# Two-layer image kernel on one core: the norm of image 1 over two rows, its mask additions over three, the last sums of image 0 ahead of the exponentials, and the residual load in the row before

## Chip, core and metric

One NeuronCore of one Trainium2 chip runs the whole batch. The metric is the device time of one launch in microseconds (us). Three runs of the kernel before give 3633.53, 3634.03 and 3636.36 us; the median is 3634.03. The profile comes from one more execution, 3639.9 us from first to last instruction (its own time is 3641.7 us).

## What is computed

The input is 32 images of 56 x 56 positions and 128 channels, float32. Two layers follow each other, each added to its own input:

```python
x = x + window_attention(group_norm(x))
x = x + fourier_ff(group_norm(x))
```

`group_norm` takes mean and variance of groups of 4 channels over a whole image. The attention cuts the image, rolled by 3 in both directions, into 8 x 8 windows of 7 x 7 positions, with 4 heads of 32; to the scores it adds a bias by relative position and a mask (-100 between regions) that differs only in the last window row and the last window column. `fourier_ff` takes a cosine transform along each axis, keeps 32 modes, mixes channels mode by mode, transforms back, adds both axes, and applies a feed-forward net of 128 -> 512 -> 128 with relu.

## The kernel before

**Work units.** An image has 8 rows of windows. The kernel's clock is the "cycle": cycle r handles window row r of the stream of 32 x 8 rows. In one cycle the attention stages of several rows stand side by side: queries and keys of row r (`attn_qk`), scores and maximum of row r, exponential and division, transposes of an earlier row, values of row r-3, projection of row r-3 (`attn_project`, which also adds the input and sends the row to a scratch tensor in DRAM), and sums of a row for the second norm (`attn_sums`). Three cycles behind the end of an image its second layer starts: statistics (`fourier_stats`), transforms, mixing, back transforms, and the feed-forward net in 7 groups of tokens at cycles 8, 9, 10, 12, 13, 14, 15 of that image (`FF_AT`), so that it runs beside the attention of the next image. The first 11 cycles (`CONV_BEGIN`) have attention only; they run through `first_rows` (L956). All later ones run through `halves_first`, `eighths`, `quarters`, `full`, `halves_last`.

**Order.** PE, ACT, DVE and POOL execute in the order in which the code is written (`tc.manual_schedule`, L999), except the setup ahead of it. SP, which issues nearly all DMAs, is ordered by a scheduler, not by the text. Buffers come from rotating pools: the attention has 4 PSUM banks (`pa`), handed out in turn, so that a matmul group waits for whoever empties the bank used four groups earlier.

**The places that the change touches.**

- `bias_and_mask(r)` (L187 to L198): 16 DVE additions of 49 x 98 that build `bm`, the table of bias plus mask. r = 0 is built at setup, r = 1 (only used by the last window row, cycle 7) in cycle 1 (L984), after the maximum of that cycle.
- `image_norm` (L315 to L368) is a generator: each `next` runs it to the next `yield`. Its pieces are: statistics on DVE and the power -0.5 on POOL (L333 to L356); the small product `nb` on DVE and the scaled weights `wn` on ACT (L358 to L362); two PE matmuls of one column that wait for `nb`, and the DVE copy of their result into `bqkv` (L364 to L367). For image 0 all of it runs ahead of cycle 0 (L1003). For image 1 all of it runs in cycle 6 (three calls in `first_rows`); for every later image in cycle 7 of the image before.
- `attn_sums` (L557): a DVE sum over `xl`, an ACT square, a DVE sum over the squares. In cycle 10 the sums of row 7 of image 0 come after `attn_exp` and `attn_divide` (L990 to L993). `fourier_stats` (L579) begins cycle 11: a DVE sum `tot` over all rows' sums, then PE matmuls with `gmean`, then a short DVE chain, then a POOL power `rstd` (L616), which ACT needs to evict the transforms (L653).
- `ff_in` (L738): allocates `res` (two buffers), issues its load from the scratch tensor (L744, L748), adds the bias `b2sb` to it on POOL (L751), then runs the first half of the feed-forward net. `ff_out` (L766) adds its result to `res` on DVE and issues the output.
- `image_bias` (L301) adds `bproj` to the image on POOL, two instructions in each of cycles 0 to 3.

Of the kernel before, what the change touches and what calls it, by code (L numbers as in the profile page):

```python
# [10 lines left out]
F32 = mybir.dt.float32  # L11
# [37 lines left out]
def swin_fourier_kernel(  # L49
# [36 lines left out]
    def conv_bank():  # L86
        return bank("pc", 4)
# [96 lines left out]
    nc.gpsimd.memset(bm, 0.0)  # L184
    rpb_f = rpb.rearrange("p (t u) y x -> p t u (y x)", u=2)

    def bias_and_mask(r):  # L187
        for t in range(2):
            for half in range(2):
                rows = slice(half * JP, half * JP + WT)  # L190
                for k, p0, p1 in ((0, 0, NP - half), (1, NP - half, NP)):
                    for p in range(p0, p1):
                        nc.vector.tensor_tensor(
                            bm[rows, r, t, p],
                            rpb_f[rows, t],
                            mask_sb[rows, r, k].unsqueeze(1).to_broadcast([WT, 2, WT]),
                            ALU.add,
                        )  # L198

    bias_and_mask(0)  # L200
    dct_w = const_load([TC, 2 * NM], dct, "dct_w")
    dct_h = const.tile([TC, 2 * NM], F32, tag="dct_h", name="dct_h")
    for r in range(0, TC, S):
# [111 lines left out]
    def image_norm(im):  # L315

        GR = C // 16

        def average(out, src):
            sums = small.tile([P, GR], F32, tag="gsums", name="gsums", bufs=2)  # L320
            nc.vector.tensor_reduce(
                sums, src.rearrange("p (g c) -> p g c", c=4), axis=AX.X, op=ALU.add
            )
            nc.vector.tensor_scalar(
                out.rearrange("p (g c) -> p g c", c=4),
                sums.unsqueeze(2).to_broadcast([P, GR, 4]),
                0.25,
                None,
                ALU.mult,
            )  # L330

        yield
        nc.vector.bn_aggr(stat[:, 0:2], im.st)  # L333

        turned = small.tile([P, 32], F32, tag="turned", name="turned", bufs=2)
        nc.vector.transpose(turned, stat)
        mean = small.tile([P, 2, 32], F32, tag="gmeans", name="gmeans", bufs=2)
        average(mean[:, 0], turned)
        nc.vector.tensor_tensor(turned, turned, mean[:, 0], ALU.subtract)
        nc.vector.tensor_tensor(turned, turned, turned, ALU.mult)  # L340
        average(mean[:, 1], turned)
        back = small.tile([P, 2, 32], F32, tag="back", name="back", bufs=2)
        nc.vector.transpose(
            back.rearrange("p k c -> p (k c)"), mean.rearrange("p k c -> p (k c)")
        )
        gm = back[:, 0, 0:1]

        nc.vector.tensor_scalar(im.xw[0][:, RT : RT + 1], gm, -1.0, None, ALU.mult)

        ve = small.tile([P, 1], F32, tag="ve", name="ve")  # L350
        nc.vector.scalar_tensor_tensor(
            out=ve, in0=back[:, 0, 1:2], scalar=1e-5, in1=back[:, 1, 0:1], op0=ALU.add, op1=ALU.add
        )
        rstd = small.tile([P, 1], F32, tag="rstd0", name="rstd0")
        nc.gpsimd.tensor_tensor(rstd, ve, mhalf, ALU.pow)
        im.w = work.tile([P, 3 * C], F32, tag="wn", name="wn")  # L356
        yield
        nb = small.tile([P, 1], F32, tag="nb0", name="nb0")  # L358
        nc.vector.scalar_tensor_tensor(
            out=nb, in0=gm, scalar=-1.0, in1=rstd, op0=ALU.mult, op1=ALU.mult  # L360
        )
        nc.scalar.mul(im.w, wqkv, rstd)  # L362
        yield
        pb = attn_bank()  # L364
        halved(pb[:, 0:1], wqkv[:, 2 * C :], nb)
        im.bias = small.tile([P, 5], F32, tag="bqkv", name="bqkv")
        nc.vector.tensor_copy(im.bias[:, 2:3], pb[:, 0:1])  # L367
        yield  # L368

# [365 lines left out]

    def ff_in(im, g):  # L738
        t0, n = sum(FF_GROUPS[:g]), FF_GROUPS[g]
        k, last = n // P, n % P  # L740
        xff = im.xf.rearrange("p r w -> p (r w)")
        scr_tok = im.scr.rearrange("h w c -> (h w) c")
        res = work.tile([P, 4, C], F32, tag="res", name="res")
        nc.sync.dma_start(  # L744
            res[:, :k], scr_tok[t0 : t0 + k * P].rearrange("(n p) c -> p n c", p=P)
        )
        if last:
            nc.sync.dma_start(res[:last, k], scr_tok[t0 + k * P : t0 + n])  # L748
        for c0, c1, m in ((0, k, P), (k, k + 1, last)):
            if m:  # L750
                nc.gpsimd.tensor_tensor(  # L751
                    res[:m, c0:c1],
                    res[:m, c0:c1],
                    b2sb[:m].unsqueeze(1).to_broadcast([m, c1 - c0, C]),
                    ALU.add,
                )
        im.res = res
        im.hid = []
        for f in range(NF):
            ph = conv_bank()  # L760
            halved(ph[:, :n], wff1[:, f * P : (f + 1) * P], xff[:, t0 : t0 + n])
            hf = work.tile([P, HB], F32, tag="hid", name="hid", bufs=NF)
            nc.scalar.activation(hf[:, :n], ph[:, :n], AF.Relu, bias=b1sb[:, f : f + 1])  # L763
            im.hid.append(hf)

    def ff_out(im, g):  # L766
        t0, n = sum(FF_GROUPS[:g]), FF_GROUPS[g]
# [67 lines left out]
    def load_back(cycle):  # L835
        for im, c in fourier(cycle):
            for width, g in back_groups(c):
                load_modes(im, width, g)

    def nothing():  # L840
        while True:
            yield
# [7 lines left out]
    def halves_first(cycle, norm):  # L850
        for im, c in fourier(cycle):
            if c == 0:
                im.stats = fourier_stats(im)
                im.cols = {}
                next(im.stats)
        last, j = row(cycle - 4)
        sums = attn_sums(last, j) if last and cycle > CONV_BEGIN else nothing()
        next(sums)
        im, i = row(cycle)
        if im:  # L860
            attn_qk(im, i, False)
        next(norm)
        next(sums)
        for im, c in fourier(cycle):
            if c in FF_AT:
                ff_in(im, FF_AT.index(c))
        for im, c in fourier(cycle):
            if c == 0:
                next(im.stats)

    def has_ff(cycle):
        return any(c in FF_AT for _, c in fourier(cycle))
# [54 lines left out]
    def halves_last(cycle, norm):  # L927
        im, i = row(cycle)
        if im:
            attn_v(im, i, cycle)  # L930
        if has_ff(cycle):
            half_columns(cycle)
        half_columns(cycle, True)
        load_back(cycle + 1)
        next_begin(cycle)
        load_first(cycle)
        next(norm)
        if row(cycle)[0]:
            attn_exp(cycle)
            attn_divide(cycle)  # L940
        im, j = row(cycle - 3)
        if im:
            last_out(cycle)
            attn_project(im, j)
        next(norm)

    def next_begin(cycle):
        b, i = divmod(cycle, NWR)
# [7 lines left out]
    def first_rows(cycle, norm):  # L956
        im, i = row(cycle)
        if im:
            attn_qk(im, i, True)
        if cycle:  # L960
            attn_exp(cycle - 1)
        im3, i3 = row(cycle - 3)
        if im3:
            attn_values(im3, i3, cycle - 3)
        im2, i2 = row(cycle - 2)
        if im2:
            attn_transpose(im2, i2, cycle - 2)
        if cycle:
            attn_divide(cycle - 1)
        if im:  # L970
            attn_scores(im, i, cycle)
            attn_max(cycle)
        if im3:
            attn_project(im3, i3)
        next(norm)
        last, j = row(cycle - 4)
        if last:
            for _ in attn_sums(last, j):
                pass
        if im:  # L980
            attn_v(im, i, cycle)
        if cycle < NWR // 2:
            image_bias(im, 2 * cycle)
        if cycle == 1:  # L984
            bias_and_mask(1)
        next(norm)
        next_begin(cycle)
        next_groups(cycle)
        if cycle == CONV_BEGIN - 1:
            attn_exp(cycle)  # L990
            attn_divide(cycle)
            for _ in attn_sums(im3, i3):
                pass  # L993
            last, j = row(cycle - 1)
            attn_transpose(last, j, cycle - 1)
        next(norm)

    ET = mybir.EngineType
    with tc.manual_schedule(engines={ET.PE, ET.Activation, ET.DVE, ET.Pool}):  # L999
        images[0] = image_begin(0)  # L1000
        for i in range(0, NWR, 2):
            image_groups(images[0], i)
        for _ in image_norm(images[0]):  # L1003
            pass
        norm = nothing()
        for cycle in range(NB * NWR + CONV_BEGIN + FF_AT[-1] - NWR + 1):
            if cycle < CONV_BEGIN:
                first_rows(cycle, norm)
# [16 lines left out]
                full(cycle)  # L1025
                halves_last(cycle, norm)
            b, i = divmod(cycle, NWR)
            norm = nothing()
            if i == (NWR - 2 if b else NWR - 3) and b + 1 < NB:
                norm = image_norm(images[b + 1])  # L1030
                next(norm)


# [60 lines left out]
```

## Time and profile before

| what | value |
|---|---|
| median of 3 runs | 3634.03 us (3633.53 to 3636.36) |
| profiled execution | 3639.9 us, mean granted PE clock 0.995 |
| PE busy | 3574.4 us, 98% |
| DVE / ACT / POOL busy | 2211.9 / 2148.1 / 1368.3 us (61 / 59 / 38%) |
| DMA | 390.31 MB, mean 107 GB/s |
| chain that ended last | PE 92%, DVE 4%, issue, ACT, POOL and DMA 1% each |

How to read it: the page gives totals, and then the span in 40 slices (91 us each), one digit of busy tenths for each engine, and the granted PE clock. The trace behind it can be asked for a stretch of time: the timeline lists instructions of an engine in order with the idle time ahead of each and what ended it (in brackets); the waits list who waited for whom, in total, times, longest; the table of windows gives each engine's busy time in a stretch and the granted clock. In all of them `pa L112 <- DVE nb L359` means that a PE instruction writing `pa` at line 112 waited for the DVE instruction at line 359 that wrote `nb`.

### The profile page before, as it was taken

To read this page: it belongs to the slowest core of one execution; us is meant where nothing else is said; L and a number is where in the kernel's file an instruction comes from. 1 tells how busy PE (TensorE), PEld (TensorE's weight loads), DVE (VectorE), ACT (ScalarE), POOL (GpSimd) and SP (SyncE) were. 2 spreads that over 40 slices of the span, in tenths; PEclk is the share of its full clock that TensorE was granted. 3 is DMA by queue.
4 is the path that set the end of the run, shared out by engine and by line. 5 is a ranking of instruction groups with operands and counts; after the bars stand their busy time and mean duration, and the time that the engine had idled before them with its cause. 6 is when DMAs were issued, how large, how long until landed. Compare 5 with 4: busy or idle time off the path is not lost.

```text
span 3639.9 us, 161666 instructions
## 1 busy us (share of the span) xinstructions
PE 3574.4 (98%) x72192; PEld 2832.6 (78%) x72192; DVE 2211.9 (61%) x4738; ACT 2148.1 (59%) x4044; POOL 1368.3 (38%) x1421
## 2 busy tenths in 40 slices
PE   7899999999999999999999999999999999999999
PEld 5677777778777787877777878777777777787776
DVE  7766666666666666666656656666566666565641
ACT  4555566655566555666556665556665556655553
POOL 5433333333343433333333434333333334343321
PEclk8999999999999999999999999999999999999999
DMA  4334434444434444334444344443444443444343
GB/s 114 86 102 112 113 96 111 108 110 111 112 97 112 112 109 116 94 110 107 113 108 111 94 114 109 113 114 94 111 108 111 110 111 94 114 109 109 97 115 98
DMA packets 687350, 390.31 MB, mean 107 GB/s; under 512 B 39967, under 2 KB 657600, under 8 KB 686400
## 3 DMA queue, kind: packets, MB, share of 16 engines
q1 hardware_dynamic: 686045, 379.65, 38.3%
q8 instruction: 568, 9.31, 1.1%
q14 instruction: 126, 1.03, 0.1%
q10 hardware_dynamic: 611, 0.32, 0.0%
HBM read 218.29 MB, written 161.48 MB: 104 GB/s over the span
## 4 chain that ended last, share of the span: by engine, by line
PE 92%; DVE 4%; issue 1%; ACT 1%; POOL 1%; DMA 1%; SPq 0%; POOLq 0%; DVEq 0%; ACTq 0%
PE pc L112 37%; PE pa L112 14%; PE pa L408 6%; PE pc L679 6%; PE pa L474 6%; PE pc L645 6%; PE pa L430 5%; PE pa L499 4%; PE pc L718 4%; PE pa L275 3%; DVE a L438 1%; DVE xf L729 0%; DVE oT L530 0%; POOL rstd L616 0%; ACT a L455 0%
## 5 line engine op out<-in xcount | busy, mean ns | idle before, releaser
L449 POOL TENSOR_TENSOR a<-a,mx 128x784 f32<-128x784 f32 x256 | 389.4, 1521 | 1427.3 <-DVE mx L448 1203.4
L112 PE MATMUL pc<-wff,hid 128*64 128x128 f32 x12544 | 740.3, 273 | 1.5 <-ACT hid L763 0.8
L112 PE MATMUL pc<-xf,wff 128*64 128x512 f32 (+2 forms) x3584 | 717.5, 539 | 1.1 <-DVE xf L729 1.0
L112 PEld LDWEIGHTS pc<-wff,hid 128*64 128x64 f32 x12544 | 702.6, 137 | 8.2 <-ACT hid L763 4.5
L460 DVE TENSOR_REDUCE sm<-a 128x16 f32<-128x784 f32 x256 | 248.2, 970 | 686.1 <-ACT a L455 682.8
L463 POOL TENSOR_TENSOR a<-a,rs 128x784 f32<-128x784 f32 x256 | 389.1, 1520 | 566.6 <-DVE rs L462 542.8
L763 ACT ACTIVATE hid<-pc,b1sb 128x512 f32<-128x512 f32 (+2 forms) x896 | 527.1, 632 | 76.6 <-PE pc L112 74.5
L112 PEld LDWEIGHTS pc<-xf,wff 128*64 128x64 f32 x3584 | 279.8, 137 | 368.0 <-issue 260.5
L379 ACT ACTIVATE q<-pa,bqkv 128x392 f32<-128x392 f32 x256 | 150.4, 587 | 473.1 <-PE pa L112 467.5
L112 PE MATMUL pa<-xw,wn 128*64 128x392 f32 (+1 forms) x2048 | 390.6, 497 | 3.7 <-DVE aT L484 2.7
L530 DVE TENSOR_SCALAR oT<-pa,bqkv 128x98 f32<-128x98 f32 (+2 forms) x768 | 171.0, 278 | 268.7 <-PE pa L499 268.6
L751 POOL TENSOR_TENSOR res<-res,b2sb 128x512 f32<-128x512 f32 (+2 forms) x256 | 264.2, 1037 | 113.5 <-DMA res<-scr 113.5
L408 PE MATMUL pa<-wn,xw 128*64 128x128 f32 x4096 | 283.6, 280 | 4.7 <-issue 3.5
L306 POOL TENSOR_TENSOR xl<-xl,bproj 112x512 f32<-112x512 f32 (+1 forms) x256 | 286.8, 1142 | 0.0
L499 PEld LDWEIGHTS pa<-aT,v 49*32 49x32 f32 x16384 | 172.9, 106 | 146.1 <-issue 127.0
L415 ACT COPY v<-pa 128x512 f32<-128x512 f32 x256 | 150.9, 589 | 228.3 <-PE pa L408 228.3
L438 DVE TENSOR_TENSOR a<-pa,bm 128x392 f32<-128x392 f32 x512 | 264.8, 559 | 25.8 <-PE pa L430 2.1
L455 ACT ACTIVATE a<-a 128x784 f32<-128x784 f32 x256 | 222.3, 869 | 97.2 <-POOL a L449 96.8
L482 ACT COPY aT<-pa 113x452 f32<-113x452 f32 x256 | 139.4, 544 | 210.4 <-PE pa L474 206.6
L408 PEld LDWEIGHTS pa<-wn,xw 128*64 128x64 f32 x4096 | 221.4, 137 | 38.6 <-issue 9.1
L112 PE MATMUL pa<-wproj,oT 128*64 128x128 f32 (+1 forms) x3584 | 248.0, 274 | 1.8 <-DVE oT L530 1.8
L448 DVE TENSOR_REDUCE mx<-a 128x16 f32<-128x784 f32 x256 | 246.3, 962 | 4.3
(91 smaller groups left out, 5583.8 us busy)
## 6 DMA issues: line engine op xcount, KB each, us to landing
zscr<-z SPq DMA_DIRECT2D x512, 112.0 KB
htok<-scr SPq DMA_DIRECT2D x256, 196.0 KB
zT<-zscr SPq DMA_DIRECT2D x192, 256.0 KB
res<-scr SPq DMA_DIRECT2D x160, 256.0 KB
out_dram<-res SPq DMA_DIRECT2D x160, 256.0 KB
scr<-xl SPq DMA_DIRECT2D x128, 224.0 KB
xl<-in_x_dram SPq DMA_DIRECT2D x32, 784.0 KB
xl<-in_x_dram SPq DMA_DIRECT2D x32, 672.0 KB
```

The costliest lines, as they stand in the source:

```text
L112: nc.tensor.matmul(dst[ps], lhsT=lhsT[:, ps], rhs=rhs, start=start, stop=stop)
L306: nc.gpsimd.tensor_tensor(piece, piece, bproj.unsqueeze(1).to_broadcast([TC, e - a, C]), ALU.add)
L408: nc.tensor.matmul(pv[hs, j * C : (j + 1) * C], lhsT=im.xw[i][:, w * WT : w * WT + JP], rhs=im.w[:, 2 * C : 3 * C], start=True, stop=True,)
L438: nc.vector.tensor_tensor(a[:, 2 * hp : 2 * hp + 2, :, 0:WT].rearrange("p u w j -> p w u j"), ps[hp][:, :RT].rearrange("p (w u j) -> p w u ...
L448: nc.vector.tensor_reduce(mx, a3, axis=AX.X, op=ALU.max)
L449: nc.gpsimd.tensor_tensor(a3, a3, mx.unsqueeze(2).to_broadcast([P, 2 * NWR, WT]), ALU.subtract)
L455: nc.scalar.activation(a3, a3, AF.Exp)
L460: nc.vector.tensor_reduce(sm, a3, axis=AX.X, op=ALU.add)
L463: nc.gpsimd.tensor_tensor(a3, a3, rs.unsqueeze(2).to_broadcast([P, 2 * NWR, WT]), ALU.mult)
L499: nc.tensor.matmul(po4[u][h * HD : (h + 1) * HD, 2 * f + e], lhsT=v[ks, 2 * f + e, h * HD : (h + 1) * HD], rhs=im.aT[i][f][ks, h, e * JP : ...
L751: nc.gpsimd.tensor_tensor(res[:m, c0:c1], res[:m, c0:c1], b2sb[:m].unsqueeze(1).to_broadcast([m, c1 - c0, C]), ALU.add,)
L763: nc.scalar.activation(hf[:, :n], ph[:, :n], AF.Relu, bias=b1sb[:, f : f + 1])
```

## The change

Four edits. (1) `bias_and_mask` takes a part (0 to 3, four additions each); table 1 is built by one part in cycle 1, one in cycle 2, two in cycle 3. (2) `image_norm` of image 0 is advanced three steps ahead of cycle 0, its last step (matmuls and copy) in cycle 0; of image 1, the statistics stay in cycle 6, the rest goes to cycle 7; `im.bias` is allocated earlier. (3) In cycle 10 the sums of row 7 go ahead of exponential and division. (4) `ff_in` is split: `load_residual` is called from `load_back`, which runs at the end of the cycle before; the POOL addition `ff_residual` is called at the end of `halves_first`.

```diff
-    def bias_and_mask(r):
-        for t in range(2):
-            for half in range(2):
-                rows = slice(half * JP, half * JP + WT)
...
+    def bias_and_mask(r, part):
+
+        t, half = divmod(part, 2)
+        rows = slice(half * JP, half * JP + WT)
...
-    def ff_in(im, g):
+    def load_residual(im, g):
         t0, n = sum(FF_GROUPS[:g]), FF_GROUPS[g]
         k, last = n // P, n % P
-        xff = im.xf.rearrange("p r w -> p (r w)")
         scr_tok = im.scr.rearrange("h w c -> (h w) c")
         res = work.tile([P, 4, C], F32, tag="res", name="res")
...
+        im.next_res = res
+
+    def ff_in(im, g):
...
+        im.res = im.next_res
...
+    def ff_residual(im, g):
...
@@ load_back(cycle)
                 load_modes(im, width, g)
+            if c in FF_AT:
+                load_residual(im, FF_AT.index(c))
@@ halves_first, at its end
             if c == 0:
                 next(im.stats)
+        for im, c in fourier(cycle):
+            if c in FF_AT:
+                ff_residual(im, FF_AT.index(c))
@@ first_rows
-        next(norm)
+        next(norm, None)
...
-        if cycle == 1:
-            bias_and_mask(1)
-        next(norm)
+        for part in {1: (0,), 2: (1,), 3: (2, 3)}.get(cycle, ()):
+            bias_and_mask(1, part)
+        if cycle == NWR - 1:
+            next(norm, None)
         next_begin(cycle)
         next_groups(cycle)
         if cycle == CONV_BEGIN - 1:
+            for _ in attn_sums(im3, i3):
+                pass
             attn_exp(cycle)
             attn_divide(cycle)
-            for _ in attn_sums(im3, i3):
-                pass
...
-        next(norm)
@@ main loop
-        for _ in image_norm(images[0]):
-            pass
-        norm = nothing()
+        norm = image_norm(images[0])
+        for _ in range(3):
+            next(norm)
```

More of the change, by code (lines that the diff above doesn't have):

```diff
@@ L185, in swin_fourier_kernel @@
     rpb_f = rpb.rearrange("p (t u) y x -> p t u (y x)", u=2)
-    def bias_and_mask(r):
-        for t in range(2):
-            for half in range(2):
-                rows = slice(half * JP, half * JP + WT)
[L191 to L200, printed above, removed]
+    def bias_and_mask(r, part):
+        t, half = divmod(part, 2)
+        rows = slice(half * JP, half * JP + WT)
+        for k, p0, p1 in ((0, 0, NP - half), (1, NP - half, NP)):
+            for p in range(p0, p1):
+                nc.vector.tensor_tensor(
+                    bm[rows, r, t, p],
+                    rpb_f[rows, t],
+                    mask_sb[rows, r, k].unsqueeze(1).to_broadcast([WT, 2, WT]),
+                    ALU.add,
+                )
+    for part in range(4):
+        bias_and_mask(0, part)
     dct_w = const_load([TC, 2 * NM], dct, "dct_w")
@@ L356, in image_norm @@
         im.w = work.tile([P, 3 * C], F32, tag="wn", name="wn")
+        im.bias = small.tile([P, 5], F32, tag="bqkv", name="bqkv")
         yield
@@ L365, in image_norm @@
         halved(pb[:, 0:1], wqkv[:, 2 * C :], nb)
-        im.bias = small.tile([P, 5], F32, tag="bqkv", name="bqkv")
         nc.vector.tensor_copy(im.bias[:, 2:3], pb[:, 0:1])
@@ L748, in ff_in @@
             nc.sync.dma_start(res[:last, k], scr_tok[t0 + k * P : t0 + n])
+        im.next_res = res
+    def ff_in(im, g):
+        t0, n = sum(FF_GROUPS[:g]), FF_GROUPS[g]
+        xff = im.xf.rearrange("p r w -> p (r w)")
+        im.res = im.next_res
+        im.hid = []
+        for f in range(NF):
+            ph = conv_bank()
+            halved(ph[:, :n], wff1[:, f * P : (f + 1) * P], xff[:, t0 : t0 + n])
+            hf = work.tile([P, HB], F32, tag="hid", name="hid", bufs=NF)
+            nc.scalar.activation(hf[:, :n], ph[:, :n], AF.Relu, bias=b1sb[:, f : f + 1])
+            im.hid.append(hf)
+    def ff_residual(im, g):
+        n = FF_GROUPS[g]
+        k, last = n // P, n % P
+        res = im.res
         for c0, c1, m in ((0, k, P), (k, k + 1, last)):
@@ L756, in ff_in @@
                 )
[L757 to L764, printed above, removed]
     def ff_out(im, g):
@@ L944, in halves_last @@
             attn_project(im, j)
-        next(norm)
+        next(norm, None)
     def next_begin(cycle):
@@ L974, in first_rows @@
             attn_project(im3, i3)
-        next(norm)
+        next(norm, None)
         last, j = row(cycle - 4)
@@ L983, in first_rows @@
             image_bias(im, 2 * cycle)
-        if cycle == 1:
-            bias_and_mask(1)
-        next(norm)
+        for part in {1: (0,), 2: (1,), 3: (2, 3)}.get(cycle, ()):
+            bias_and_mask(1, part)
+        if cycle == NWR - 1:
+            next(norm, None)
         next_begin(cycle)
@@ L989, in first_rows @@
         if cycle == CONV_BEGIN - 1:
+            for _ in attn_sums(im3, i3):
+                pass
             attn_exp(cycle)
             attn_divide(cycle)
-            for _ in attn_sums(im3, i3):
-                pass
             last, j = row(cycle - 1)
             attn_transpose(last, j, cycle - 1)
-        next(norm)
     ET = mybir.EngineType
@@ L1027, in swin_fourier_kernel @@
             b, i = divmod(cycle, NWR)
-            norm = nothing()
             if i == (NWR - 2 if b else NWR - 3) and b + 1 < NB:
                 norm = image_norm(images[b + 1])
-                next(norm)
+                next(norm, None)
 def _constants():
```

## The prediction

> **What bounds the kernel now.** I read three views in this order: the 40 slices, the table of windows, and PE's waits. The slices of the page show where there is anything to win:
>
> ```profile
> PE   7899999999999999999999999999999999999999
> PEclk8999999999999999999999999999999999999999
> ```
>
> Only the first two slices (182 us) have a PE that is visibly idle or below full clock. The table of windows (length, then PE busy first) puts numbers on the middle:
>
> ```profile
> 1000.00:1900.00 900.00, 894.68 (x18214) 713.40 (x18214) 555.21 (x1184) 539.07 (x1014) 343.91 (x356) 1.00 0.40 108
> 1900.00:2800.00 900.00, 896.52 (x18262) 712.71 (x18260) 557.89 (x1190) 542.94 (x1025) 343.89 (x357) 1.00 0.40 108
> ```
>
> PE is busy 99.4 to 99.6% of these at clock 1.00. So from about 204 us on PE is the bound. From 240 to 3500 us PE's waits add to 10.1 us for some 29 images. The time before 204 us holds the rest; the same waits over the whole span name the edits' places:
>
> ```profile
> PE pa L112 <- DVE nb L359: 10.3, 3, 4.7
> ...
> PE pa L112 <- DVE tot L581: 4.0, 1, 4.0
> ...
> PE pa L112 <- DVE aT L484: 2.7, 1, 2.7
> ```
>
> One long wait for each startup edit: nb (norms of images 0 and 1), tot (second norm of image 0), aT (behind the mask additions). But in this stretch DVE is nearly full too (22 to 25 us of each 30 from 30 to 120 us), so a wait of PE is worth only what DVE can follow.
>
> **What the Trainium skill says.** "SBUF — State Buffer", section "SBUF: two separate sides": a DVE instruction with two SBUF inputs and a GpSimd instruction that reads SBUF exclude each other; whoever starts first holds the shared port for its whole instruction. The mask additions (rpb and mask, both SBUF) are of this kind. The trace agrees: with POOL idle 8 took 1.48 us (24.47), 0.19 each; in cycle 1 they met POOL's L449 and L306. Chain of waits (start, length, what), then POOL's timeline:
>
> ```profile
> 33.77 3.07 DVE bm L193 x4
> 36.85 1.49 DVE bm L193 x4
> 38.36 0.77 DVE bm L193 x4
> 39.13 0.78 DVE bm L193 x4
> ```
> ```profile
> 33.92 1.57 POOL L449 TENSOR_TENSOR a<-a,mx 128x784 f32<-128x784 f32 x1 [0.38 <-DVE mx L448]
> 35.45 2.26 POOL L306 TENSOR_TENSOR xl<-xl,bproj 112x512 f32<-112x512 f32 x2
> ```
>
> The first four take 3.1 us, the last eight 0.77 per four once POOL is done at 37.7. "TensorE: Matmul & The Clock Gate", section "What's actually happening": PE falls to half clock after an idle window of about 3.4 us and is back after a busy one. Here it shows after PE's idle 4.41 us at 77.1: 77.1 to 86.9 has clock 0.53.
>
> **The change part by part.** I compared the built programs' instruction order, engine by engine.
>
> Edit 4, residual: SP has the same DMAs in the same order with the same kinds of wait before and after, because SP's order is the scheduler's, which had already put each load ahead as far as the two buffers allow (in the tail each load is issued 2.3 us after the output that frees its buffer). POOL differs only once per image: the power L616 now stands ahead of the residual addition L751 (1.28 us), which so waits for the statistics too. Waits of that power, 220 to 3500 us:
>
> ```profile
>   DVE ve L612: 54.7, 29
> ```
>
> POOL was idle for 1.9 us before each of the 29, so the addition never held it back: no gain. The addition then comes some 4 us later (428.4 for 424.74); behind it on POOL stands L449 of the next maximum, which waits another 4.4 us for DVE (at 432.80), and ff_out's DVE addition comes at 437.7. No loss. DMAs: none moves. Value 0; ends -1.2 (the only other wait of ACT's L653 for that power, 5.1 us in two, 3.9 of them in image 0) and +1.
>
> Edit 2, image 0: the two one-column matmuls leave the space before the first queries. Those start at 18.43, and wn, which they need, ends at 18.38: no gain. DVE's first mask table waits for a DMA until 24.47 anyway: 0. The two matmuls go in front of the values of cycle 0, where PE is later idle 1.05 us: 0 (ends -0.4, +0.7).
>
> Edit 1, mask additions. Cycle 1 keeps 4 instead of 16: DVE goes on at 36.84 instead of 39.95, -3.1. DVE's timeline from there, before:
>
> ```profile
> 42.86 0.97 DVE L448 TENSOR_REDUCE mx<-a 128x16 f32<-128x784 f32 x1
> 43.74 0.66 DVE L530 TENSOR_SCALAR oT<-pa,bqkv 128x98 f32<-128x98 f32 x3
> 44.73 0.63 DVE L484 COPY aT<-pa 113x452 f32<-113x452 f32 x1 [0.32 <-PE pa L474]
> 46.36 0.97 DVE L460 TENSOR_REDUCE sm<-a 128x16 f32<-128x784 f32 x1 [1.01 <-ACT a L455]
> ...
> 49.56 0.55 DVE L547 TENSOR_TENSOR xl<-pa,xl 112x384 f32<-112x384 f32 x1
> 51.70 0.67 DVE L530 TENSOR_SCALAR oT<-pa,bqkv 128x98 f32<-128x98 f32 x3 [1.58 <-PE pa L499]
> ```
>
> Cycle 2: its four stand right behind the maximum, with L449 and two L306 released on POOL at that moment, exactly the picture of 33.77: 3.1 us. So oT stays at 43.8, and the 1.33 us of idle (0.32 + 1.01) is what is won: the maximum of cycle 3 comes 1.4 earlier, at 47.3. Cycle 3: eight stand behind xl, while POOL runs L449 and L306 (3.8 us from 48.4 on); one gets in at each POOL boundary, the last five behind it at 0.19: they end at 53.3, where oT was at 51.70: +1.6. Waiting for that oT: PE's scores (52.88 before), and through them everything. From 51.7 to 72.7 PE and DVE have no idle but DVE's 0.34 at 60.07: +1.3 remains. Ends: -3.1 (no lock in cycles 2 and 3, additions in the idle time) and +4 (PE's new idle, 2.8 us at 41.6 and 2.3 us at 51.7, makes a further row run cold).
>
> Edit 2, image 1. Before, PE's timeline, then DVE's:
>
> ```profile
> 77.12 0.38 PE L112 MATMUL pa<-nb,wqkv 128*64 128x1 f32 x4 [4.41 <-DVE nb L359]
> 77.33 2.89 PE L112 MATMUL pa<-xw,wn 128*64 128x392 f32 x8
> ```
> ```profile
> 81.24 0.67 DVE L530 TENSOR_SCALAR oT<-pa,bqkv 128x98 f32<-128x98 f32 x3 [3.55 <-PE pa L499]
> ```
>
> After, the queries of cycle 7 start at 72.7, values are done at 75.0 (1.49 + 0.81 of warm rows), so oT starts when DVE has done statistics and sums, 76.9: -4.3. The matmuls now wait for nb in cycle 7, where it stands behind maximum and xl: from oT 76.9 by the row's own durations (0.67, 0.63, 0.96, 0.25, 1.04, 0.97, 0.55 with their overlaps) nb is ready at 81.9, while PE is done with the values at 80.8: a new wait of 1.1 us. Queued behind it on PE are the queries of cycle 8. They end at 83.6, values at 84.4, next oT 84.4 instead of 89.22: -4.8. ACT's wn (0.62) falls into its 3.08 us of idle. Ends: -3.4 (those queries cold, 2.89 for 1.49) and -5.6 (DVE alone sets it, 83.6).
>
> Edit 3, cycle 10, DVE before:
>
> ```profile
> 109.72 0.97 DVE L460 TENSOR_REDUCE sm<-a 128x16 f32<-128x784 f32 x1 [1.08 <-ACT a L455]
> ...
> 112.63 0.61 DVE L581 TENSOR_REDUCE tot<-part 112x64 f32<-112x448 f32 x1
> ```
>
> The two sums (0.63, 0.67) fill that 1.08; the square on ACT (0.61, free from 107.7) ends before the exponential's 108.82. sm moves to 109.9, tot to 111.8: -0.9 (ends 0 and -1.1).
>
> Sum: 0 + 0 + 1.3 - 4.8 - 0.9 = **-4.4 us**. It shifts the start of all PE-bound work. It is worked out on the profiled span of 3639.9 us; the runs without a profile have a median 5.9 us below. I carry the difference over to them: 3634.0 - 4.4 = 3629.6, -0.12%.
>
> **The rivals.**
> - *A, the additions fit into the idle time.* Speaks for it: they need only 0.77 and 1.5 us unlocked, against 1.33 and 1.58 idle. Against: POOL's work begins at the very same maximum. -3.1 - 4.8 - 0.9 = -8.8: 3625.2.
> - *B, the clock takes the gain back (slower).* In cycles 3 to 6 PE waits for the displaced oT long enough to fall to half clock, row after row. A cold row costs 3.3 us (77.1 to 86.9 against a warm row: 1.40 + 0.22 + 0.47 + 0.18 + 0.67 + 0.33). It decides from two cold rows on; four give +13.2 - 4.4 = +8.8: 3642.8. Against it: PE's new gaps are 2.3 to 2.8 us, and rows 4 to 6 have more PE work.
> - *C, the split of the residual does act,* through a wait that the order doesn't show: the bounds above are per run, so about -1.2 or +1: 3628.4 or 3630.6, hardly to be told apart. That edit 4 doesn't do what it says is thus my main case.
>
> **How the numbers follow.** Main case (with C) 0.68, about 3627 to 3633 by the ends of its parts; A 0.24; B 0.08. Range 3624.5 to 3634.5: above it lies B, 0.08; below it half of A, 0.12 (where a warmer PE adds to it). A measurement can tell about 0.2% (7.3 us) from no change, so faster means below 3626.8: A, 0.24; slower means above 3641.3: most of B, 0.06; the rest, 0.70, within.
>
> **What would show it.** PE's waits: nb's 4.4 us at 77 gone, one of about 1 us a row later; tot's 4.0 down to about 3; the DVE timeline with 3 us for the four additions of cycle 2 and over 4 for the eight of cycle 3; first transform 4 to 5 us earlier; from 240 us on the same length as before; POOL's waits for res unchanged. I am wrong if the middle stretch changes length, or if the additions run at 0.19 each (then A).

## The result: slower, and the profile after

The changed kernel takes 3664.61 us (median; 3663.67 to 3665.70), the kernel before 3635.2 on the same chip: ratio 1.0079, 95% interval 1.0061 to 1.0096, some 22 to 35 us. The forecast was 3629.6, with a range of 3624.5 to 3634.5. The profiled execution spans 3663.2 us.

The slices of the page show nothing of it; the loss is too evenly spread for them:

```profile
PE   6899999999999999999999999999999999999999
PEclk9999999999999999999999999999999999999999
```

The table of windows for the two middle stretches (length; PE busy, PEld, DVE, ACT, POOL; clock) shows it:

```profile
1000.00:1900.00 900.00, 888.31 (x18082) 705.39 (x18080) 560.80 (x1181) 535.76 (x1009) 342.78 (x354) 1.00 0.40 108
1900.00:2800.00 900.00, 890.17 (x18164) 704.03 (x18160) 561.04 (x1182) 539.60 (x1016) 341.92 (x353) 1.00 0.40 108
```

PE lost 6.4 us of busy time in each of these (894.68 and 896.52 before), at full clock, and DVE gained 5.6 and 3.2 although it executed fewer instructions (1181 for 1184, 1182 for 1190). So the loss lies in the PE-bound part, where I had written "no loss", and it has to do with DVE. The prediction had named a change of this stretch as a sign that it is wrong. PE's waits of the whole span name it (total, times, longest):

```profile
PE pc L646 <- DVE xf L730: 29.2, 25, 1.2
...
PE pa L431 <- DVE oT L531: 6.1, 3, 3.4
...
PE pa L112 <- DVE nb L361: 4.0, 2, 2.8
PE pa L112 <- DVE tot L582: 3.2, 1, 3.2
```

The first line is new. In the trace of before the same wait is:

```profile
PE pc L645 <- DVE xf L729: 0.2, 1, 0.2
```

It was 0.2 us, and is 29.2 now, up to 1.2 us at a time, 25 times, about once per image. L646 is the first transform of the Fourier layer (L645 before), waiting for a PSUM bank that DVE empties at L730. Why DVE is late there is seen by laying one such place of the two traces side by side. Before, DVE and POOL (start, length, instruction, idle ahead of it):

```profile
428.41 0.16 DVE L618 SCALAR_TENSOR_TENSOR shift<-ms,rstd 128x1 f32<-128x1 f32 x1 [0.66 <-POOL rstd L616]
428.49 0.66 DVE L530 TENSOR_SCALAR oT<-pa,bqkv 128x98 f32<-128x98 f32 x3
```
```profile
424.74 1.29 POOL L751 TENSOR_TENSOR res<-res,b2sb 128x512 f32<-128x512 f32 x1
427.83 0.55 POOL L616 TENSOR_TENSOR rstd<-ve,mhalf 128x1 f32<-128x1 f32 x1 [1.80 <-DVE ve L612]
```

After, DVE, POOL and PE:

```profile
431.41 1.22 DVE L619 SCALAR_TENSOR_TENSOR shift<-ms,rstd 128x1 f32<-128x1 f32 x1 [0.66 <-POOL rstd L617]
432.56 0.66 DVE L531 TENSOR_SCALAR oT<-pa,bqkv 128x98 f32<-128x98 f32 x3
433.14 1.02 DVE L439 TENSOR_TENSOR a<-pa,bm 128x392 f32<-128x392 f32 x2
434.09 1.73 DVE L730 TENSOR_TENSOR xf<-pc,xf 128x448 f32<-128x448 f32 x4
```
```profile
430.83 0.55 POOL L617 TENSOR_TENSOR rstd<-ve,mhalf 128x1 f32<-128x1 f32 x1 [3.04 <-DVE ve L613]
431.35 1.27 POOL L769 TENSOR_TENSOR res<-res,b2sb 128x512 f32<-128x512 f32 x1
```
```profile
434.75 2.44 PE L646 MATMUL pc<-dct_w,xl 112*64 112x64 f32 x76 [1.21 <-DVE xf L730]
```

`shift`, a product of one element per partition, takes 1.22 us instead of 0.16. It waits for POOL's power, and in the same moment POOL, done with the power, starts the residual addition that edit 4 has put behind it: 431.35 to 432.62, and `shift` ends at 432.63. It multiplies `ms` by `rstd`, two tensors in SBUF. This is the case that the prediction cites from the Trainium skill, "SBUF — State Buffer" (in its section "Who interferes with whom": "A DVE instruction with two SBUF inputs contends with a GpSimd instruction that reads SBUF"). Behind `shift` on DVE stand oT, the scores' addition and xf, and PE has nothing in hand to bridge 1.06 us. Over the trace:

```profile
L619 DVE SCALAR_TENSOR_TENSOR shift<-ms,rstd x32: 160/1222/1241, 116.3 to 3552.1; 128x1 f32<-128x1 f32 x32
```

(shortest/median/longest in ns.) That is 31.9 us more of DVE in all, and 31.9 of the 36.6 us by which DVE's busy time grew. The trace of before held a warning that I overlooked: one instance of 32, in the last image, where a residual addition (3528.40 to 3529.68) stands behind the power already. There `shift` took 1.27 us:

```profile
L618 DVE SCALAR_TENSOR_TENSOR shift<-ms,rstd x32: 158/159/1271, 115.6 to 3528.4; 128x1 f32<-128x1 f32 x32
```

### The profile page after: what moved, and what is told of

The parts are those of the page before. It is cut to its first block, busy times and chain, and to the rows that moved or that the text cites. A ratio compares the mean times of both kernels' runs of the same rounds, so it can differ in the third digit from the quotient of the medians.

```text
span 3663.2 us, 161699 instructions
## 1 busy us (share of the span) xinstructions
PE 3572.4 (98%) x72192; PEld 2823.3 (77%) x72192; DVE 2248.5 (61%) x4738; ACT 2148.5 (59%) x4044; POOL 1369.9 (37%) x1421
## 4 chain that ended last, share of the span: by engine, by line
PE 82%; DVE 9%; POOL 3%; issue 3%; ACT 2%; DMA 1%; SPq 0%; POOLq 0%; DVEq 0%; ACTq 0%
PE pc L112 33%; PE pa L112 13%; PE pc L680 6%; PE pc L646 6%; PE pa L409 5%; PE pa L431 5%; PE pa L475 4%; PE pa L500 4%; PE pc L719 3%; PE pa L276 3%; DVE xf L730 2%; DVE a L439 2%; POOL a L450 1%; POOL a L464 1%; DVE sm L461 1%
## 5 line engine op out<-in xcount | busy, mean ns | idle before, releaser
L769 POOL TENSOR_TENSOR res<-res,b2sb 128x512 f32<-128x512 f32 (+2 forms) x256 | 264.4, 1038 | 103.6 <-DMA res<-scr 103.6
L431 PE MATMUL pa<-k,q 64*64 64x98 f32 x8192 | 236.4, 251 | 14.7 <-DVE oT L531 6.1
L797 DVE TENSOR_TENSOR res<-pc,res 128x512 f32<-128x512 f32 (+3 forms) x257 | 138.6, 550 | 181.4 <-PE pc L112 138.7
```

What stands on the lines that cost most here:

```text
L431: nc.tensor.matmul(ps[hp][HALVES[e], pr * 2 * WT : (pr + 1) * 2 * WT], lhsT=q[cs, w * WT : w * WT + JP], rhs=k_sb[cs, :, w], start=True, s ...
L769: nc.gpsimd.tensor_tensor(res[:m, c0:c1], res[:m, c0:c1], b2sb[:m].unsqueeze(1).to_broadcast([m, c1 - c0, C]), ALU.add,)
```

## The experiments

Three explanations stand against each other. *Lock theory*: what is described above; `shift`, which reads two SBUF tensors, is shut out until the POOL instruction that started just before it has ended. *Row theory*: the addition comes later in the row, and holds up what stands behind it on POOL, or its reader on DVE. *Startup theory*: edits 1 to 3 cost the time. Times of the first four stand beside the kernel before on the same chip, 3638.88 us; those of the last four beside 3636.52.

**The addition ahead of the statistics again**, all else as changed:

```diff
+        for im, c in fourier(cycle):
+            if c in FF_AT:
+                ff_residual(im, FF_AT.index(c))
         for im, c in fourier(cycle):
             if c == 0:
                 next(im.stats)
-        for im, c in fourier(cycle):
-            if c in FF_AT:
-                ff_residual(im, FF_AT.index(c))
```

> The changed kernel, but in each cycle the residual addition on POOL stands ahead of the statistics again, as before the change; edits 1 to 3 and the split of ff_in stay. Lock theory (the small product shift on DVE reads two SBUF tensors, rstd and ms, at the very moment at which POOL starts the residual addition, and is shut out for that whole instruction): shift back from 1222 to 160 ns in all 32 images, PE's wait for xf (29.2 us) gone, time 3636 us. Row theory (the residual addition coming later holds up what stands behind it on POOL or its reader on DVE): also 3636 us. Startup theory (edits 1 to 3 cost the time): stays at 3664 us.

Measured 3641.33 us (3638.51 to 3645.06), ratio 1.0003 (0.9995 to 1.0011): the whole loss is gone. `shift` and PE's wait in its trace:

```profile
L619 DVE SCALAR_TENSOR_TENSOR shift<-ms,rstd x32: 158/159/163, 115.2 to 3525.9; 128x1 f32<-128x1 f32 x32
```
```profile
PE pc L646 <- DVE xf L730: 0.6, 4, 0.2
```

The startup theory falls: with its three edits in place the kernel is level with the one before. Lock and row stay.

**`shift` with one tensor input**, order untouched:

```diff
-        nc.vector.scalar_tensor_tensor(
-            out=shift, in0=ms[:, 0:1], scalar=-SQRT_S, in1=rstd, op0=ALU.mult, op1=ALU.mult
-        )
+        nc.vector.tensor_scalar(shift, ms[:, 0:1], rstd, -SQRT_S, ALU.mult, ALU.mult)
```

> The changed kernel with shift as a tensor_scalar: rstd is a per-partition scalar instead of a second tensor input, the order on all engines is unchanged, so the residual addition still comes after the power. Lock theory: shift about 160 ns beside the running addition, PE's wait for xf gone, time 3636 us. Row theory and startup theory: 3664 us, since neither the addition's place nor the startup has changed.

Measured 3640.81 us (3637.07 to 3645.15), ratio 1.0003 (0.9995 to 1.0011). The timelines of DVE and POOL at the same place of this kernel:

```profile
428.88 0.21 DVE L619 TENSOR_SCALAR shift<-ms,rstd 128x1 f32<-128x1 f32 x1 [0.66 <-POOL rstd L617]
```
```profile
428.29 0.55 POOL L617 TENSOR_TENSOR rstd<-ve,mhalf 128x1 f32<-128x1 f32 x1 [3.04 <-DVE ve L613]
428.81 1.28 POOL L767 TENSOR_TENSOR res<-res,b2sb 128x512 f32<-128x512 f32 x1
```

The addition still follows the power at once, and still runs 1.28 us; `shift` runs through beside it, in 0.21 us rather than the 0.16 that I had expected. PE's wait is nearly gone:

```profile
PE pc L644 <- DVE xf L728: 4.3, 22, 0.2
```

Row theory asked for 3664, so it falls. The form reads the same two tensors, but `rstd` as a scalar of each partition, not as a second tensor.

**The swap alone, in the kernel before** (the POOL addition taken out of `ff_in` and called behind the statistics; load and all else as before):

> The kernel before with one thing of the change: the residual addition on POOL called after the statistics (its load stays in ff_in; SP keeps its order). Lock theory and row theory: all of the loss, 3663 us, shift 1222 ns. Startup theory: 3635 us.

Measured 3663.97 us (3660.89 to 3666.34), ratio 1.0064 (1.0050 to 1.0078), so 25 us lost (18 to 28). `shift` and PE's wait:

```profile
L618 DVE SCALAR_TENSOR_TENSOR shift<-ms,rstd x32: 159/1222/1235, 115.3 to 3551.1; 128x1 f32<-128x1 f32 x32
```
```profile
PE pc L645 <- DVE xf L729: 30.2, 29, 1.2
```

One moved instruction per image is the whole loss, within the intervals (25 us here, 29 for the changed kernel on another chip).

**The addition in four pieces** for the first token group, order as changed:

```diff
+        parts = [(0, k, P), (k, k + 1, last)]
+        if g == 0:
+            parts = [(c, c + 1, P) for c in range(k)]
-        for c0, c1, m in ((0, k, P), (k, k + 1, last)):
+        for c0, c1, m in parts:
```

> The changed kernel with the residual addition of the first token group of each image (the one behind the power) in four POOL instructions of 128x128 instead of one of 128x512; order unchanged. Lock theory: the lock is held for one instruction, so shift waits for the first quarter alone, 0.4 to 0.5 us instead of 1.22, and the loss falls to a third or less: 3639 to 3645 us. Row theory: four instructions take longer together, the addition ends later still: 3664 us or more.

Measured 3642.66 us (3638.47 to 3645.43), ratio 1.0009 (1.0001 to 1.0017). In its trace, `shift`, PE's wait and the four pieces:

```profile
L619 DVE SCALAR_TENSOR_TENSOR shift<-ms,rstd x32: 159/405/409, 113.3 to 3530.0; 128x1 f32<-128x1 f32 x32
```
```profile
PE pc L646 <- DVE xf L730: 8.9, 23, 0.4
```
```profile
427.10 1.70 POOL L772 TENSOR_TENSOR res<-res,b2sb 128x128 f32<-128x128 f32 x4
```

The four take 1.70 us together, longer than the one, and yet `shift` waits for the first quarter alone and PE's wait falls from 29.2 to 8.9 us. So what costs is the length of the one POOL instruction that `shift` meets. The time is 3.8 us above the kernel before (0.4 to 6.2), of 25 in the experiment above: below a third of the loss, as expected.

The power in front of `shift` marks where each image's second layer begins, so its first and last start in a trace part the startup from the recurring work. Before, changed, first, second, third and fourth experiment:

```profile
L616 POOL TENSOR_TENSOR rstd<-ve,mhalf x32: 547/547/550, 115.0 to 3527.8; 128x1 f32<-128x1 f32 x32
L617 POOL TENSOR_TENSOR rstd<-ve,mhalf x32: 549/550/551, 115.7 to 3551.5; 128x1 f32<-128x1 f32 x32
L617 POOL TENSOR_TENSOR rstd<-ve,mhalf x32: 549/550/551, 114.7 to 3525.3; 128x1 f32<-128x1 f32 x32
L617 POOL TENSOR_TENSOR rstd<-ve,mhalf x32: 548/549/551, 115.3 to 3527.6; 128x1 f32<-128x1 f32 x32
L616 POOL TENSOR_TENSOR rstd<-ve,mhalf x32: 548/549/552, 114.7 to 3550.6; 128x1 f32<-128x1 f32 x32
L617 POOL TENSOR_TENSOR rstd<-ve,mhalf x32: 548/550/552, 112.8 to 3529.4; 128x1 f32<-128x1 f32 x32
```

From first to last it is 3412.8 us before, 3435.8 in the changed kernel and 3435.9 with the swap alone, the same 23 us more; with the addition ahead of the statistics again it is 3410.6. The first start also shows how far a single trace can be trusted for the startup. Four of these kernels have the same startup code (changed, first, second, fourth), and theirs lie at 115.7, 114.7, 115.3 and 112.8.

**Edit 1 alone** in the kernel before. From here on I read the startup by a marker: the start of the first POOL power of `fourier_stats`. By the scatter just shown, a difference of one or two us between two traces decides nothing.

> The kernel before with edit 1 alone (mask additions 4, 4 and 8 in cycles 1, 2 and 3). Marker: the start of the first power on POOL in fourier_stats (115.0 us before), which all startup work precedes. Lock theory (the additions, two SBUF inputs, meet POOL's L449 and L306 in every one of the three cycles): the four of cycle 2 take 3 to 4 us, the eight of cycle 3 over 4 us, marker 3 to 4 us later, 118 to 119. Idle theory (they fill DVE's idle time at 0.19 us each): marker at 112.

Marker 115.9 us, a single run 3637.39. DVE's and POOL's timelines in cycles 2 and 3 of this kernel:

```profile
40.23 3.98 DVE L193 TENSOR_TENSOR bm<-rpb,mask 49x98 f32<-49x98 f32 x4
...
49.01 4.57 DVE L193 TENSOR_TENSOR bm<-rpb,mask 49x98 f32<-49x98 f32 x8
53.61 0.67 DVE L531 TENSOR_SCALAR oT<-pa,bqkv 128x98 f32<-128x98 f32 x3
```
```profile
40.28 1.59 POOL L450 TENSOR_TENSOR a<-a,mx 128x784 f32<-128x784 f32 x1 [0.38 <-DVE mx L449]
41.83 2.27 POOL L307 TENSOR_TENSOR xl<-xl,bproj 112x512 f32<-112x512 f32 x2
```

Four take 4 us, eight 4.6: locked in every cycle, 11.7 us of DVE (with the 3.15 of cycle 1) for what took 6.23 in one piece. That refutes the idle theory. The marker missed my 118 to 119. It is 0.9 us later than before, near the prediction's +1.3, but that is within the scatter of the marker.

**Edit 2 alone** in the kernel before:

> The kernel before with edit 2 alone (norm of images 0 and 1 over two rows). The prediction's step: marker (first power, 115.0 before) 4.8 us earlier, 110.2. Lock theory: nb, a scalar_tensor_tensor with two SBUF inputs, now follows the projection's addition and meets POOL's subtraction of the maximum; it takes about 1.3 us instead of 0.15, PE waits 2.5 to 3 us for it and falls to half clock; marker only about 2 us earlier, 113.

Marker 113.9, 1.1 us earlier than before where the prediction has 4.8; a single run 3639.0. DVE's and PE's timelines in cycles 7 and 8:

```profile
82.77 1.29 DVE L360 SCALAR_TENSOR_TENSOR nb<-back,rstd 128x1 f32<-128x1 f32 x1
```
```profile
84.21 0.35 PE L112 MATMUL pa<-nb,wqkv 128*64 128x1 f32 x4 [2.84 <-DVE nb L360]
84.35 2.93 PE L112 MATMUL pa<-xw,wn 128*64 128x393 f32 x8
```

`nb` is the same kind of product, and meets POOL's L449: 1.29 us for 0.15. PE waits 2.84 us instead of the 1.1 that I had worked out, and its next matmuls take 2.93 us, at half clock, where the next kernel's take 1.54.

**Edits 2 and 3, nb with rstd as scalar:**

```diff
-        nc.vector.scalar_tensor_tensor(
-            out=nb, in0=gm, scalar=-1.0, in1=rstd, op0=ALU.mult, op1=ALU.mult
-        )
+        nc.vector.tensor_scalar(nb, gm, rstd, -1.0, ALU.mult, ALU.mult)
```

> The kernel before with edits 2 and 3, nb written as a tensor_scalar with rstd as per-partition scalar; no change to the residual or the masks. Lock theory: nb takes 0.2 us, PE waits 1.0 to 1.6 us for it, marker at about 110 (109 to 111), time 4 to 5 us below the kernel before on the same chip, 0.9987 of it. If the lock is not what held nb: PE's wait stays near 2.8 us and the marker at 112.

Marker 110.5; 3633.26 us (3630.52 to 3635.53), ratio 0.9990 (0.9983 to 0.9997). PE, same place:

```profile
82.97 0.28 PE L112 MATMUL pa<-nb,wqkv 128*64 128x1 f32 x4 [1.75 <-DVE nb L360]
83.09 1.54 PE L112 MATMUL pa<-xw,wn 128*64 128x393 f32 x8
```

The time is 3.3 us below the kernel before (1.1 to 6.2), where I expected 4 to 5. The lock is off (nb 0.20 us) and the wait is shorter by the same 1.1 us. It is 1.75, a little above the expected 1.0 to 1.6: nb was ready at 82.8 instead of 81.9, because oT of that row began at 77.8 instead of the 76.9 that the prediction worked out.

The matmuls behind ran at full clock here, but that isn't shown to come from the new form. In the trace of the fourth experiment, where nb is locked for 1.29 us as in edit 2 alone, they did too:

```profile
82.03 1.93 PE L409 MATMUL pa<-wn,xw 128*64 128x128 f32 x16
85.37 0.28 PE L112 MATMUL pa<-nb,wqkv 128*64 128x1 f32 x4 [1.41 <-DVE nb L361]
85.49 1.54 PE L112 MATMUL pa<-xw,wn 128*64 128x393 f32 x8
```

There the half clock fell on the values ahead of the wait (1.93 us, 1.04 in edit 2 alone), which made them end later and the wait shorter. So with the same code the half clock can fall on another row, which is likely a part of the marker's scatter.

**No meeting at all:**

```diff
+    bias_and_mask(0, 0, nc.vector)
+    bias_and_mask(1, 0, nc.vector)
+    bias_and_mask(0, 1, nc.vector)
...
-        if cycle == 1:
-            bias_and_mask(1)
+        if cycle == NWR - 2:
+            bias_and_mask(1, 1, nc.gpsimd)
...
+        if im.b < 2:
+            yield
```

(The arguments are table, half of the partitions, engine; the yield stands behind nb, so that nb runs at the end of cycle 6 and wn in cycle 7; the last window row's mask has a tile of its own.)

> As e7, with nb computed at the end of cycle 6, and with the mask additions kept away from POOL: half of table 1 on DVE at setup while it waits for a DMA, the other half on POOL in cycle 6, from a mask tile of its own (its four loads are issued by ACT). shift and the residual are as in the kernel before. Lock theory: DVE's 6.2 us in cycle 1 are gone without coming back elsewhere, no wait of PE for nb; marker 4 to 7 us earlier than in e7, 103 to 107, time 8 to 11 us below the kernel before, 0.997 to 0.9978. If startup gains are taken back later by the attention chain between 130 and 204 us: marker as said, but the time no better than e7's.

Marker 105.0; 3627.33 us (3624.42 to 3627.94), ratio 0.9970 (0.9959 to 0.9982): 9.2 us faster than the kernel before (6.5 to 15), and so, across chips, faster than the changed one too. POOL's eight additions, in time that POOL had idle:

```profile
74.07 2.73 POOL L199 TENSOR_TENSOR bm<-rpb,mask 49x98 f32<-49x98 f32 x8
```

The marker came 10.0 us earlier and the time fell by 9.2: the startup gain was not taken back later. The run doesn't tell how much of the further gain over the experiment before belongs to the masks and how much to nb's earlier place.

## Why the prediction was wrong, step by step

- **Edit 4, residual, is the step that failed.** It said "Value 0; ends -1.2 ... and +1" and "No loss". Measured: 25 us for the swap alone (18 to 28), which accounts for the 29 us (22 to 35) of the whole change. Its facts held: SP's order didn't move, no load moved (POOL's waits for res: 113.5 us before, 103.6 after), the power had not been held back. But I asked only what is queued behind the addition on POOL and who reads it. I didn't ask what DVE does while it runs, although the rule for that stood a paragraph above and was applied to the masks. In the order before, the addition was over 2.4 us before `shift` began (at the place shown). And the end "+1" was taken per launch, where the place recurs in 31 images: 1.06 us each, the growth of `shift`, gives 33 as an upper estimate, of which 23 to 29 were measured.
- **The sum of the startup edits failed too**, by less. The first and second experiment have all startup edits without the recurring loss; they lie between 1.8 us below and 4.0 us above the kernel before, which excludes the -4.4. The mean of the four markers is 114.6, of the two with the startup of before 114.8: the startup edits together gained about nothing.
- **Edit 1**, +1.3: its size isn't shown (+0.9 by the marker, within the scatter). The mechanism is shown: the additions of cycle 2 took 4.0 us instead of 3.1, those of cycle 3 4.6 where "over 4" was foreseen. Cycle 2 was not "exactly the picture" of cycle 1: the first addition began only 0.05 us ahead of POOL's subtraction (40.23 against 40.28), in cycle 1 it was 0.23 us (33.69 against 33.92), so fewer ran before POOL did.
- **Edit 2**, -4.8: -1.1 by the marker of edit 2 alone. The mis-sized term is the new wait, 1.1 us worked out, 2.84 measured; 1.1 of it is the same lock, on nb. The queries behind it ran cold (at half clock), the case of the step's end "-3.4". With nb as scalar, edits 2 and 3 together give -4.5 by the marker, against -5.7 summed, and -3.3 by the times.
- **Edit 3**, -0.9: PE's wait for tot fell from 4.0 to 3.2 us, -0.8.
- **Rivals.** A (additions in idle time): refuted. B (slower by cold rows in cycles 3 to 6): right in the sign alone; the recurring loss has clock 1.00. C was the right part of the change, without its price.

## What to carry to other kernels

When an instruction moves on POOL, look at what DVE executes at its new time, not only at the queues and the readers. Two instructions that wait for the same event start together each time; here 0.06 us apart at the place shown, in 31 of 32 images. In these runs a small DVE instruction that reads two SBUF tensors lasted until the POOL instruction that it met had ended. If one of the two is a value per partition, it can be passed as the scalar, as `shift` and `nb` were; that form takes 0.20 us alone, where the other takes 0.15. A cost at a place that recurs is bounded per recurrence, before it is called zero.

## What the runs showed of the hardware

- The lock holds for 128x1 products as for wide additions: 159 ns alone, 1222 beside a POOL addition of 1.27 us, 405 beside four of 0.43 each.
- A per-partition scalar in SBUF isn't shut out: 214 ns (median; longest 216) beside the running addition, image after image.
- Spreading 16 locked additions over three cycles nearly doubled their cost on DVE (6.23 to 11.7 us): in each cycle the first ones wait out POOL's instructions one by one.
- The length of a gap alone didn't tell whether half clock follows or how long it lasts. In the fourth experiment the clock was 0.50 from 81.0 to 84.3 us, though PE had been busy for 2.13 of the 3.40 us before and its longest wait there was 0.72. In the kernel before, PE was busy for 9.78 of the 9.80 us from 77.1 on, at a mean clock of 0.53; the prediction had it back at full clock after one busy window of about 3.4.
